# Raw steps loaded ahead, a split pool and a first cell with a pool of its own in a four-layer graph kernel

## The chip, the cores and the metric

The kernel runs on one core of a Trainium2 chip. The metric is the device time of one execution in microseconds (us). Engines are named as in the profile: PE (TensorE, matmuls; PEld its weight loads), DVE (VectorE), ACT (ScalarE), POOL (GpSimd) and SP (SyncE, which here only issues DMAs). A name followed by "q" (SPq) is the issuing queue of that engine.

## What is computed

A graph of 2708 nodes with 256 features passes through four layers; each adds the layer's output to its input and normalizes the row. The adjacency matrix `adj` is sparse in values, dense in storage (2708 x 2708, float32). Cut to what matters here:

```python
x = layernorm(x + adj @ (x * W0))                      # layer 0
# layer 1: attention with 4 heads of 64
e    = leaky_relu(src[:, None] + dst[None, :], 0.2)
attn = softmax(where(adj > 0, e, -9e15))
out1 = layernorm(attn @ h)
x    = layernorm(x + out1)
# layer 2: two GRU cells over sums and attention with signs
node_support = (adj - diag) @ x
edge_output  = gru(node_support, x, edge_Wih, edge_Whh)
edge_support = mean over 3 heads of (softmax by signs of adj) * adj @ (x @ gat_W)
node_output  = gru(edge_support, x, node_Wih, node_Whh)
x = layernorm(x + diag * edge_output + diag * node_output)
# layer 3
x = layernorm(x + concat(x, adj @ (x @ nW.T) / deg) @ lW.T)
```

The change touches the last part of layer 1 and the first part of layer 2: the sums `(adj - diag) @ x` and the first GRU cell that uses them.

## The kernel before

The nodes make 22 row tiles of 128 (the last has 20 rows). Features are kept as two parts of 128. Tiles of memory come from pools that are stacked on a left and a right side; a pool that is opened after another was closed takes its place, and what writes first into the new tile waits for the last use of the old one. Each engine's queue runs in order. A scheduler decides the order within each engine from the order of the program and the dependencies; `issue_after` holds some of it fixed (the p's on DVE behind each other, the head and total products on PE behind each other).

**Layer 1.** The loop at line 790 goes over groups of two spans of columns (`spans` are of up to 512 columns); the last group has 384 + 276 = 660 columns. Inside, the loop at line 813 goes over the two pairs of heads (q = 0 and 1), and for each pair over blocks of two tiles. DVE makes the attention weights `p` (line 844) from `fall_b`, a table of 128 x 2 x 1024 values for this group and pair that SP loads (line 417), from `rise` and from the mask; nine buffers (`held`) rotate. PE then multiplies: `heads` (line 820) gives the weighted sums in `acc`, `totals` (line 830) the denominators in `den`. Blocks alternate which of the two comes first.

`fall_b` is one of two buffers of the pool `fallp`, popped from the list `falls`; behind a group's last use a new tile of the same tag is appended and loaded for the next group.

Between the products, `step` (line 798) advances the ends of the tiles of the group before, two tiles (a pair) at a time. These are generators; each `yield` gives way to the next part of the products. `layer1_end` (line 687) turns the sums with PE transposes (lines 698, 699), divides by the denominators (DVE L709/L712, ACT L716), takes the variance and its power on POOL (L684), and adds and normalizes twice (DVE L731, L734; ACT L747, L748). `layer1_logits` (line 752) then transposes the new rows (PE L760), copies them out of PSUM (ACT L762), stores them to memory (POOL's DMA queue, L770), gives way once, and multiplies them with a small matrix (`pm`, PE L777: 128 x 3 outputs) whose result ACT copies to `u_all` (L781).

The last group has no group behind it that could cover its ends: they run from line 889 on, between the first raw steps.

**Raw sums.** `raw_sums` (line 354) is a generator for one "raw", a column block of 226 columns out of each half of the nodes (six raws; the last is 224 wide); `ahead` chains all of them. A raw has MH = 11 steps c, one for each pair of row tiles. A step loads four quarters of the adjacency matrix into a tile `pa` (`load_pairs`, line 259: five DMAs in raw 0, six in raw 1, all issued by SP), clears the diagonal where it falls (`clear_own`, POOL L286), and calls `seven` (line 309): four additions on DVE (L315 to L318) and seven products of block matrices on PE (L328, 14 matmuls, as the profile counts two for each float32 product). In raw 0 the step also forms `xq` from x (`quarter_sums`, DVE L294 to L297). Step c thus needs x of the tiles 2c and 2c + 1, and the last steps of raw 0 need x of layer 1's last group. At the end of a raw `gathered` (line 332) makes `supt`.

**Logits and first cell.** Lines 899 to 1055 form layer 2's attention logits and their statistics, with raw steps drawn from `ahead` between (`next(ahead)`). Their small tiles are in the pool `tail`, right side. At the end, PE transposes the statistics (L1044), ACT copies them (L1048) and POOL's queue stores them to `st_d` (L1054). Then the pools of layer 1 are closed, and the cells begin at line 1105: the pool `e_work` holds the weights `wih` and `whh`, the input `xt2` (two buffers) and what the cell works with. For each raw r the loop first draws raw steps until two raws are ready ahead, then loads the input and calls `gru_t` (line 1068): per half (j), 24 gate matmuls (L1081) into four PSUM banks, ACT's gate functions (L1086), DVE's combination (L1093 to L1099).

The stage behind it (line 1336 on) shares the engines with the later cells: ACT forms attention weights from the statistics that were stored (`st` loaded by SP at L1144; ACT L1347, L1350), DVE multiplies them with the adjacency block (L1351).

Of the kernel before, what the change touches and what calls it, by code (L numbers as in the profile page):

```python
# [9 lines left out]
F32 = mybir.dt.float32  # L10
# [9 lines left out]
P = 128  # L20
# [7 lines left out]
def kernel(  # L28
# [323 lines left out]
    xq = []  # L352

    def raw_sums(pool, ps, keep, r):

        a, w = raws[r]
        m = [ps.tile([P, 2, W // 2], F32, tag=nm, name=nm) for nm in ("m1", "m26", "m75", "m43")]
        m[0] = m[0][:, 0]
        for c in range(MH):
            pa = pool.tile([P, 2, 2, w], F32, tag="pa", name="pa", bufs=5)  # L360
            load_pairs(raws, r, c, pa)
            clear_own(raws, r, c, pa)
            if r == 0:
# [33 lines left out]

    keep_stack, fall_stack, acc_stack, ps_t_stack, xq_stack, eblk_stack, ps_s_stack = (ExitStack() for _ in range(7))
    keep = keep_stack.enter_context(pool("l1keep"))
    if True:  # L400
# [12 lines left out]
        if True:  # L413
# [39 lines left out]
            with pool("l0", 2) as l0:  # L453
# [165 lines left out]
                beta_b = keepr.tile([P, F], F32, name="beta_b")  # L619
                fallp = fall_stack.enter_context(pool("fallp", 2, side="right"))  # L620
                falls = [fallp.tile([P, 2, 2 * W], F32, tag="fall_b", name="fall_b") for _ in range(H // 2)]
                held = [fallp.tile([P, 2 * W], F32, name=f"p{i}", bufs=1) for i in range(4)]
# [42 lines left out]
            if True:  # L665
# [85 lines left out]

                def layer1_logits(pair):

                    pt = ps_t.tile([P, 4, P], F32, tag="tr", name="tr")
                    at = (2 * GT + 1 + 2 * (pair[0][-1] // 2 % 2)) * F
                    xt = turn[:, at : at + 2 * F].rearrange("p (i f n) -> p i f n", i=2, f=FC)
                    for i, a in enumerate(pair):
                        t, n = a[0], sz(a[0])
                        for f in range(FC):
                            nc.tensor.transpose(pt[:, i * FC + f, :n], xs[t][:n, f * P : (f + 1) * P], ident[:n, :n])  # L760
                    if all(sz(a[0]) == P for a in pair):
                        nc.scalar.copy(xt.rearrange("p i f n -> p (i f) n"), pt)  # L762
                    else:
                        for i, a in enumerate(pair):
                            n = sz(a[0])
                            nc.scalar.copy(xt[:, i, :, :n], pt[:, i * FC : (i + 1) * FC, :n])
                    for i, a in enumerate(pair):
                        t, n = a[0], sz(a[0])
                        at, _, d = [p for p in xt_d if p[0] <= t * P][-1]
                        nc.gpsimd.dma_start(d[:, :, t * P - at : t * P - at + n], xt[:, i, :, :n])  # L770
                    yield

                    pm = ps_t.tile([P, 4, P], F32, tag="tr", name="pm")
                    for i, a in enumerate(pair):
                        n = sz(a[0])
                        for f in range(FC):
                            nc.tensor.matmul(  # L777
                                pm[:n, i, :K], xt[:, i, f, :n], uw[:, f, :], start=(f == 0), stop=(f == FC - 1)
                            )
# [10 lines left out]
                for g in range(0, len(spans), 2):  # L790
# [7 lines left out]
                    def step(c):  # L798
                        with tc.issue_after(product.ins) if g == 0 else nullcontext():
                            for s in list(steps):  # L800
                                if next(s, s) is s:
                                    steps.remove(s)

                        if q == 0 and c % 5 == 1 and len(halves) < len(ended):
                            halves.append(layer1_end(l1, ended[len(halves)]))
                            next(halves[-1])
                            steps.append(itertools.islice(halves[-1], 2))

                        if q == 1 and c % 5 == 0 and c // 5 < len(halves):
                            steps.append(itertools.chain(halves[c // 5], [None], layer1_logits(ended[c // 5])))  # L810
                            next(steps[-1])

                    for q in range(H // 2):
# [21 lines left out]

                        fall_b = falls.pop(0)
                        for b, c0 in enumerate(range(0, NT, 2)):
# [18 lines left out]
                        if g + 2 < len(spans):  # L856
                            falls.append(fallp.tile([P, 2, 2 * W], F32, tag="fall_b", name="fall_b"))
                            for i in range(len(spans[g + 2 : g + 4])):
                                load_fall(falls[-1], g + 2 + i, q, nc.sync)
                        got = []  # L860
# [28 lines left out]
                turns = [itertools.chain(layer1_end(tail, a), [None], layer1_logits(a)) for a in ended]  # L889
                k = 0  # L890
# [7 lines left out]

                u_parts = tail.tile([P, NT, CT], BF16, name="u_parts", bufs=1)
                nc.gpsimd.memset(u_parts, 0.0)  # L900
                rest = u_all
                for i in range(SPLITS):
                    part = u_parts[:, :, i * K : (i + 1) * K]
                    nc.vector.tensor_copy(part, rest)
                    if i + 1 < SPLITS:
                        r = tail.tile([P, NT, K], F32, tag="u_left", name="u_left")
                        nc.vector.tensor_tensor(r, rest, part, ALU.subtract)
                        rest = r
# [15 lines left out]
                def turned_sums(acc, groups, cols, copies):  # L924

                    w, full = width(*spans[groups[0]]), len(groups) * cols
                    parts = tail.tile([P, W], F32, tag="parts", name="parts")
                    nc.scalar.copy(parts[:full, :w], acc[:full, :w])
# [22 lines left out]
                first = -STEP  # L951
                own_u = tail.tile([P, NT, K], F32, name="own_u", bufs=1)
                nc.vector.scalar_tensor_tensor(
# [5 lines left out]

                inside = tail.tile([P, NT, K], F32, name="inside", bufs=1)  # L960
                nc.vector.tensor_scalar(inside, logit, first - STEP / 2, None, ALU.is_ge)
# [14 lines left out]
                centres = centre[:, None].to_broadcast([P, NT, BANDS, K])  # L976
                q_parts = tail.tile([P, NT, 2 * CT], BF16, name="q_parts", bufs=1)
                nc.gpsimd.memset(q_parts, 0.0)
# [747 lines left out]
```

## Time and profile before

| | |
|---|---|
| times of three runs | 1844.74, 1841.54, 1843.25 us; median 1843.25 |
| the profiled execution | 1845.3 us; span from first to last instruction 1843.5 us |
| mean granted clock of PE in it | 0.997 of full speed |
| PE busy, 529 to 556 / 556 to 582 / 582 to 612 us | 27.00 of 27 / 24.45 of 26 / 26.78 of 30 |
| DVE busy in the same stretches | 26.04 / 15.24 / 26.60 |
| granted clock in the same stretches | 1.00 / 0.93 / 1.00 |
| layer 1's last pm before the passage, and the first tile transpose | 581.97 and 582.89 us |
| first cell's gate matmuls | begin at 708.69 us |

The profile is of one execution. A line of the timeline or of a group names the line of the kernel, the engine, the operation with its output and input, its shape, and how often it came (x); in square brackets stands how long the engine was idle before it and what released it. "L777" is line 777 of the kernel. Releasers are inferred; an end of a matmul is modelled, as matmuls are pipelined, so a short wait of PE can be hidden in a longer matmul, and "issue" is idle time with no releaser in the profile. The granted clock is the share of the full clock that TensorE was allowed in that stretch.

### The profile page before, as it was taken

The page shows a single profiled execution, that of the slowest core. Times are in us where ns is not written, and L with a number is a line of the kernel's source. Part 1 is how long each engine was busy: PE and PEld are TensorE (multiplying, and loading weights), DVE is VectorE, ACT ScalarE, POOL GpSimd, SP SyncE. Part 2 cuts the span into 40 slices and gives each one's busy share as a digit, 9 for nine tenths or more (in the row PEclk, how much of TensorE's full clock was granted, in tenths as well). Part 3 has the DMA queues.
Part 4 walks back from the last instruction along what each step waited for, and adds up shares of the span by engine and source line. Part 5 has one row for each costly group of instructions (what it writes and reads, how often), then busy time and mean ns, then how long its engine had stood idle before and what let it go on. Part 6 is the DMA issues. An engine that isn't in the chain of part 4 may idle for free.

```text
span 1843.5 us, 23048 instructions
## 1 busy us (share of the span) xinstructions
PE 1819.7 (99%) x7512; PEld 1038.2 (56%) x7512; DVE 1267.9 (69%) x2242; ACT 699.0 (38%) x1449; POOL 287.3 (16%) x441
## 2 busy tenths in 40 slices
PE   9999999999999999999999999999999999999997
PEld 7888842233455886788444444444445556655555
DVE  5333399998797655654558888686887768945664
ACT  4444420033144203111555655555654556321011
POOL 1322211011113411000002000110200202121211
PEclk9999999999999999999999999999999999999999
DMA  8343310000103667755557666453654445634774
GB/s 302 121 163 126 126 53 26 24 1 21 33 7 78 147 145 193 170 134 123 175 136 207 178 175 173 125 151 110 170 161 125 124 108 148 174 99 120 202 172 124
DMA packets 435711, 237.34 MB, mean 129 GB/s; under 512 B 184459, under 2 KB 422444, under 8 KB 433148
## 3 DMA queue, kind: packets, MB, share of 16 engines
q1 hardware_dynamic: 423534, 210.76, 42.3%
q0 software_dynamic: 7696, 20.50, 3.5%
q10 hardware_dynamic: 4350, 4.50, 0.7%
q8 instruction: 62, 1.02, 0.2%
q14 instruction: 69, 0.57, 0.1%
HBM read 223.00 MB, written 12.66 MB: 128 GB/s over the span
## 4 chain that ended last, share of the span: by engine, by line
PE 91%; DMA 3%; DVE 2%; ACT 1%; SPq 1%; issue 1%; POOL 0%; POOLq 0%; DVEq 0%
PE m L328 42%; PE acc L820 11%; PE acc L214 8%; PE bank L1206 8%; PE den L830 6%; PE gate L1081 4%; PE bank L1182 3%; PE bank L1249 2%; PE acc L519 2%; PE pm L425 1%; DMA strip<-in_adj_t_dram 1%; SPq L275 1%; PE m L1453 1%; DMA p<-in_adj_t_dram 1%; PE pq L1002 1%
## 5 line engine op out<-in xcount | busy, mean ns | idle before, releaser
L844 DVE SCALAR_TENSOR_TENSOR p<-fall_b,rise,mask 128x1024 f32<-128x1024 f32 (+1 forms) x264 | 288.5, 1154 | 28.8 <-PE den L830 17.4
L1347 ACT ACTIVATE p<-st,e_neg 128x1024 f32<-128x1024 f32 (+1 forms) x198 | 197.5, 1040 | 193.0 <-PE m L328 188.1
L328 PE MATMUL m<-s,xq 128*128 128x512 f32 (+3 forms) x660 | 230.1, 467 | 0.0
L820 PE MATMUL acc<-p,h 128*64 128x512 f32 (+2 forms) x1056 | 209.2, 546 | 0.0
L214 PE MATMUL acc<-turn,strip 128*128 128x257 f32 x792 | 182.8, 381 | 1.8 <-DMA strip<-in_adj_t_dram 1.7
L328 PE MATMUL m<-p,xq 128*128 128x512 f32 (+1 forms) x396 | 183.0, 544 | 0.2
L315 DVE TENSOR_TENSOR s<-p 128x512 f32<-128x512 f32 (+3 forms) x132 | 82.1, 622 | 146.8 <-PE m L328 115.1
L1350 ACT ACTIVATE p<-p 128x1024 f32<-128x1024 f32 (+1 forms) x198 | 179.0, 943 | 0.2
L328 PE MATMUL m<-p,x 128*128 128x512 f32 (+1 forms) x396 | 167.6, 542 | 0.3 <-DVE supt L345 0.3
L328 PEld LDWEIGHTS m<-s,xq 128*128 128x128 f32 x660 | 124.5, 190 | 76.1 <-issue 59.5
L1351 DVE TENSOR_TENSOR p<-p,blk 128x1024 f32<-128x1024 f32 (+1 forms) x132 | 142.9, 1102 | 34.4 <-ACT p L1350 23.4
L214 PEld LDWEIGHTS acc<-turn,strip 128*128 128x128 f32 x792 | 147.2, 189 | 23.7 <-DMA strip<-in_adj_t_dram 3.0
L820 PEld LDWEIGHTS acc<-p,h 128*64 128x64 f32 x1056 | 72.3, 137 | 129.3 <-issue 121.6
L328 PE MATMUL m<-s,x 128*128 128x512 f32 (+3 forms) x330 | 127.0, 467 | 0.0
L328 PEld LDWEIGHTS m<-p,xq 128*128 128x128 f32 x396 | 74.6, 190 | 76.9 <-issue 61.0
L328 PEld LDWEIGHTS m<-p,x 128*128 128x128 f32 x396 | 74.8, 190 | 75.5 <-issue 60.9
L457 DVE TENSOR_SCALAR mask<-strip 128x2816 fp8e4<-128x2816 f32 (+5 forms) x40 | 40.0, 1030 | 110.3 <-DMA strip<-in_adj_t_dram 110.2
L830 PE MATMUL den<-p,h 128*32 128x512 f32 (+2 forms) x1056 | 111.5, 551 | 0.0
L286 POOL TENSOR_TENSOR blk<-blk,offdiag 128x128 f32<-128x128 f32 (+3 forms) x50 | 29.1, 588 | 375.2 <-DMA blk<-in_adj_t_dram 326.3
L472 ACT ACTIVATE below<-strip 128x384 bf16<-128x384 f32 x132 | 78.4, 594 | 17.8 <-DMA strip<-in_adj_t_dram 14.4
L328 PEld LDWEIGHTS m<-s,x 128*128 128x128 f32 x330 | 62.0, 190 | 39.0 <-issue 34.6
L316 DVE TENSOR_TENSOR p<-p 128x512 f32<-128x512 f32 (+3 forms) x132 | 81.9, 620 | 2.4
(286 smaller groups left out, 2642.4 us busy)
## 6 DMA issues: line engine op xcount, KB each, us to landing
strip<-in_adj_t_dram SPq DMA_DIRECT2D x19, 1408.0 KB, 6.0
blk<-in_adj_t_dram SPq DMA_DIRECT2D x88, 256.0 KB, 3.5
blk<-in_adj_t_dram SPq DMA_DIRECT2D x88, 192.0 KB, 4.1
pa<-in_adj_t_dram SPq DMA_DIRECT2D x110, 128.0 KB, 2.7
turn<-in_adj_t_dram SPq DMA_DIRECT2D x44, 256.0 KB, 3.2
blk<-in_adj_t_dram SPq DMA_DIRECT2D x88, 128.0 KB, 2.7
p<-in_adj_t_dram SPq DMA_DIRECT2D x88, 128.0 KB, 2.8
turn<-in_adj_t_dram SPq DMA_DIRECT2D x44, 192.0 KB, 3.2
```

What stands on the lines that cost most here:

```text
L214: at = nc.tensor.matmul(acc, s[:, c, :n], rhs(c), start=(c == 0), stop=(c == NT - 1))
L315: nc.vector.tensor_tensor(s1, a21, a22, ALU.add)
L316: nc.vector.tensor_tensor(a21, a21, a11, ALU.subtract)
L328: nc.tensor.matmul(dst[:, :w], lt, rt, start=start and not (one_bank and i in (3, 4, 6)), stop=stop and not (one_bank and i in (1, 2, 5)))
L472: nc.scalar.activation(below[:, : (hi - lo) * P], s[:, lo:hi].rearrange("p c n -> p (c n)"), AF.Relu, scale=-1.0, accum_out=negative[:, BE ...
L820: at = nc.tensor.matmul(acc[s][i * HD : (i + 1) * HD, :ws], hs[c][:, 2 * q + i, :HD], ps[i][:, p0 : p0 + ws], **flags,)
L830: at = nc.tensor.matmul(den[j : j + CT, :ws], hs[c][:, 2 * q + i, HD + 1 - CT :], ps[i][:, p0 : p0 + ws], **flags,)
L844: nc.vector.scalar_tensor_tensor(p[:, :w], fall_b[:, i, :w], rise[:, c, 2 * q + i : 2 * q + i + 1], mask[:, c, at : at + w], ALU.max, ALU. ...
L1206: nc.tensor.matmul(g[:, :w], lt, rt, start=(q == 0), stop=(q == len(terms) - 1))
L1347: nc.scalar.activation(p[:, :, :w], st_k[:, :, :w], AF.Relu, scale=-1.0, bias=e_neg[:, at, k : k + 1])
L1350: nc.scalar.activation(p[:, :, :w], p[:, :, :w], AF.Exp, scale=-1.0)
L1351: nc.vector.tensor_tensor(p[:, :, :w], p[:, :, :w], blk[:, i, :, :w], ALU.mult)
```

## The change

- The two buffers of `fallp` become two tiles in two pools, `spare` for the first pair of heads and `fallp` for the second; each is loaded again for each group (`falls[q]`) instead of being allocated again.
- In the last group, after the first pair of heads, the first buffer isn't loaded again. Its first part becomes two views of the shape of `pa` (`early`), and raw steps 0 and 1 of raw 0 are loaded and cleared there at once (`loaded`). Of five buffers in rotation, two are these views from then on, and the pool of `pa` has three instead of five. For the cells, two tiles of `e_work` take the views' place.
- `layer1_logits` gives way twice instead of once before `pm` when it is called in the last group.
- The pool `tail` is split: the tiles of the logits' first part, the ends of layer 1 and several of the logits' sums come from a second pool `sums`, the rest (the band tiles, `centre`, `total`, `shift`, `den`, `drows`, `sr`) stays.
- `wih`, `whh` and the first `xt2` are in a pool `e_in` of their own, opened before `e_work`; the second `xt2` stays in `e_work`. For a raw with a cell, the input is loaded before the raw steps are drawn, not behind them.

The instructions are the same in number and kind apart from these places. In the order of PE, the cell's first gate matmuls come after 2 products of raw sums behind the transpose `pl` (L1061) where they came after 23, and the raw sums that no longer stand before it follow after the first half of the cell.

```diff
+    early, loaded = [], {}
+
+    def raw_loaded(pool, r, c):
+        if (r, c) in loaded:
+            return loaded.pop((r, c))
+        k = (r * MH + c) % 5
+        pa = early[k] if k < len(early) else pool.tile([P, 2, 2, RW], F32, tag="pa", name="pa", bufs=3)
+        load_pairs(raws, r, c, pa)
+        clear_own(raws, r, c, pa)
+        return pa
...
         for c in range(MH):
-            pa = pool.tile([P, 2, 2, w], F32, tag="pa", name="pa", bufs=5)
-            load_pairs(raws, r, c, pa)
-            clear_own(raws, r, c, pa)
+            pa = raw_loaded(pool, r, c)
...
-                fallp = fall_stack.enter_context(pool("fallp", 2, side="right"))
-                falls = [fallp.tile([P, 2, 2 * W], F32, tag="fall_b", name="fall_b") for _ in range(H // 2)]
+                spare = spare_stack.enter_context(pool("spare", side="right"))
+                fallp = fall_stack.enter_context(pool("fallp", side="right"))
+                falls = [a.tile([P, 2, 2 * W], F32, name=f"fall{q}") for q, a in enumerate((spare, fallp))]
...
-                def layer1_logits(pair):
+                def layer1_logits(pair, apart=1):
...
-                    yield
+                    for _ in range(apart):
+                        yield
...
-                            steps.append(itertools.chain(halves[c // 5], [None], layer1_logits(ended[c // 5])))
+                            steps.append(itertools.chain(halves[c // 5], [None], layer1_logits(ended[c // 5], 1 + (g + 2 >= len(spans)))))
...
-                        fall_b = falls.pop(0)
+                        fall_b = falls[q]
...
                         if g + 2 < len(spans):
-                            falls.append(fallp.tile([P, 2, 2 * W], F32, tag="fall_b", name="fall_b"))
                             for i in range(len(spans[g + 2 : g + 4])):
-                                load_fall(falls[-1], g + 2 + i, q, nc.sync)
+                                load_fall(fall_b, g + 2 + i, q, nc.sync)
+                        elif q == 0:
+                            free = fall_b.rearrange("p i n -> p (i n)")[:, : 8 * RW]
+                            early += list(free.rearrange("p (k j h n) -> k p j h n", k=2, j=2, h=2))
+                            for c in range(2):
+                                loaded[0, c] = raw_loaded(None, 0, c)
...
                 tail = fall_stack.enter_context(pool("tail", 2, side="right"))
+                sums_pool = fall_stack.enter_context(pool("sums", 2, side="right"))
...
-                logit = tail.tile([P, NT, K], F32, name="logit", bufs=1)
+                logit = sums_pool.tile([P, NT, K], F32, name="logit", bufs=1)
...
-    for q in (fall_stack, mask_stack, ps_t_stack):
+    for q in (fall_stack, spare_stack, mask_stack, ps_t_stack):
         q.close()
...
-    with pool("e_work") as ework, pool("ps_g", 4, space=PSUM, side="right") as ps_g:
-        wih, whh = weights(ework, "wih", e_wih), weights(ework, "whh", e_whh)
+    with pool("e_in") as e_in, pool("e_work") as ework, pool("ps_g", 4, space=PSUM, side="right") as ps_g:
+        early.clear()
+        inputs = [e_in.tile([P, FC, 2 * RW], F32, name="xt2")]
+        wih, whh = weights(e_in, "wih", e_wih), weights(e_in, "whh", e_whh)
+        inputs.append(ework.tile([P, FC, 2 * RW], F32, name="xt2"))
         for r, (a, w) in enumerate(raws):
+            if r not in left:
+                xt = inputs[r % 2][:, :, : 2 * w]
+                for h in range(2):
+                    load_columns(xt[:, :, h * w : (h + 1) * w], xt_d, h * NH + a, w)
+            if r == 1:
+                early[:] = [ework.tile([P, 2, 2, RW], F32, name=f"pa{i}") for i in range(2)]
             while len(edges) < min(r + 2, len(raws)):
                 next(ahead)
             if r not in left:
-                xt = ework.tile([P, FC, 2, w], F32, tag="xt2", name="xt2", bufs=2)
-                for h in range(2):
-                    load_columns(xt[:, :, h], xt_d, h * NH + a, w)
                 yt = ework.tile([P, FC, 2 * w], F32, tag="yt", name="yt")
-                gru_t(ps_g, ework, yt, edges[r], xt.rearrange("p f h w -> p f (h w)"), 2 * w, wih, whh, b_edge)
+                gru_t(ps_g, ework, yt, edges[r], xt, 2 * w, wih, whh, b_edge)
```

More of the change, by code (lines that the diff above doesn't have):

```diff
@@ L395 @@
     nc.gpsimd.memset(mask[:, :, N:], 0.0)
-    keep_stack, fall_stack, acc_stack, ps_t_stack, xq_stack, eblk_stack, ps_s_stack = (ExitStack() for _ in range(7))
+    keep_stack, spare_stack, fall_stack, acc_stack, ps_t_stack, xq_stack, eblk_stack, ps_s_stack = (ExitStack() for _ in range(8))
     keep = keep_stack.enter_context(pool("l1keep"))
@@ L887 @@
                 ahead = itertools.chain.from_iterable(raw_sums(eblk, ps_s, xqp, r) for r in range(len(raws)))
-                turns = [itertools.chain(layer1_end(tail, a), [None], layer1_logits(a)) for a in ended]
+                turns = [itertools.chain(layer1_end(sums_pool, a), [None], layer1_logits(a)) for a in ended]
                 k = 0
@@ L897 @@
                     k += 1
-                u_parts = tail.tile([P, NT, CT], BF16, name="u_parts", bufs=1)
+                u_parts = sums_pool.tile([P, NT, CT], BF16, name="u_parts", bufs=1)
                 nc.gpsimd.memset(u_parts, 0.0)
@@ L905 @@
                     if i + 1 < SPLITS:
-                        r = tail.tile([P, NT, K], F32, tag="u_left", name="u_left")
+                        r = sums_pool.tile([P, NT, K], F32, tag="u_left", name="u_left")
                         nc.vector.tensor_tensor(r, rest, part, ALU.subtract)
@@ L926, in turned_sums @@
                     w, full = width(*spans[groups[0]]), len(groups) * cols
-                    parts = tail.tile([P, W], F32, tag="parts", name="parts")
+                    parts = sums_pool.tile([P, W], F32, tag="parts", name="parts")
                     nc.scalar.copy(parts[:full, :w], acc[:full, :w])
@@ L951 @@
                 first = -STEP
-                own_u = tail.tile([P, NT, K], F32, name="own_u", bufs=1)
+                own_u = sums_pool.tile([P, NT, K], F32, name="own_u", bufs=1)
                 nc.vector.scalar_tensor_tensor(
@@ L958 @@
                 nc.vector.tensor_scalar(e_neg, logit, -1.0, None, ALU.mult)
-                inside = tail.tile([P, NT, K], F32, name="inside", bufs=1)
+                inside = sums_pool.tile([P, NT, K], F32, name="inside", bufs=1)
                 nc.vector.tensor_scalar(inside, logit, first - STEP / 2, None, ALU.is_ge)
@@ L976 @@
                 centres = centre[:, None].to_broadcast([P, NT, BANDS, K])
-                q_parts = tail.tile([P, NT, 2 * CT], BF16, name="q_parts", bufs=1)
+                q_parts = sums_pool.tile([P, NT, 2 * CT], BF16, name="q_parts", bufs=1)
                 nc.gpsimd.memset(q_parts, 0.0)
```

## The prediction

> **What bounds the kernel now.** I read the page's engine shares first, then PE's waits over the stretch that the change touches, then PE's timeline there, then the queues behind those waits.
>
> ```profile
> PE 1819.7 (99%) x7512; PEld 1038.2 (56%) x7512; DVE 1267.9 (69%) x2242; ACT 699.0 (38%) x1449; POOL 287.3 (16%) x441
> ...
> PE 91%; DMA 3%; DVE 2%; ACT 1%; SPq 1%; issue 1%; POOL 0%; POOLq 0%; DVEq 0%
> ```
>
> PE is busy 1819.7 of 1843.5 us, so only 23.8 us are idle in all. The change removes no matmul; it can win idle PE time, time hidden inside modelled matmul ends, and a lowered clock. PE's waits from 500 to 700 us:
>
> ```profile
> PE m L328 <- issue: 1.6, 2, 1.3
> PE pm L777 <- ACT turn L762: 1.5, 1, 1.5
> PE tr L698 <- ACT turn L716: 0.6, 1, 0.6
> PE m L328 <- DVE pa L316: 0.5, 1, 0.5
> PE m L328 <- POOL pa L286: 0.4, 1, 0.4
> ```
>
> All five lie in two places: one pm wait at 558, and the passage from layer 1 to the raw steps (583 to 612). PE's timeline at the first, then one-us windows over it (length, PE busy, granted clock, DMA):
>
> ```profile
> 556.53 1.35 PE L830 MATMUL den<-p,h 128*32 128x320 f32 x16
> 559.43 1.26 PE L777 MATMUL pm<-uw,turn 128*128 128x3 f32 x8 [1.55 <-ACT turn L762]
> 560.62 2.50 PE L830 MATMUL den<-p,h 128*32 128x320 f32 x16
> ```
>
> ```profile
> 558.00:559.00 1.00, 0.00 (x0) 1.00 0.00 0
> ...
> 560.00:561.00 1.00, 1.00 (x9) 0.57 0.12 41
> 561.00:562.00 1.00, 1.00 (x12) 0.50 0.70 213
> 562.00:563.00 1.00, 1.00 (x8) 0.50 0.03 8
> 563.00:564.00 1.00, 1.00 (x8) 0.72 0.00 0
> ```
>
> The reader sees a 1.55 us wait, and then the same 16 den matmuls taking 2.50 us instead of 1.35, at half clock. The copy L762 was ready at 556.53, but ACT held it behind L747, which waited until 557.4 for POOL's power; it ended at 559.38.
>
> At the second place (PE, then SP's queue):
>
> ```profile
> 585.96 1.19 PE L328 MATMUL m<-pa,x 128*128 128x226 f32 x4 [0.40 <-POOL pa L286]
> ...
> 607.18 0.62 PE L328 MATMUL m<-pa,xq 128*128 128x226 f32 x2 [1.26 <-issue]
> ...
> 611.84 0.60 PE L760 MATMUL tr<-ident,x 128*128 128x128 f32 x4
> ```
>
> ```profile
> 582.21 47.92 SPq L275 DMA_DIRECT2D pa<-in_adj_t_dram  x88
> ```
>
> SP issues loads back to back: 47.92/88 = 0.54 us each, five a step in raw 0, so 2.7 us a step; PE's step is 14 matmuls of 0.191 (four start 0.77 apart in the timeline) = 2.68. PE can't gain on SP, which starts only when layer 1's memory is free. No view says more for the next 300 us: PE's waits from 700 to 900 are 1.0 us.
>
> **The change, part by part.**
>
> *Second advance for pm (apart = 2 in the last group).* One totals part of the next block (1.28 to 1.35) moves from behind pm to before it: it fills 557.88 to 559.16, and pm then waits at most 559.38 − 559.16 = 0.22. Its p's were ready at 555.9 (DVE idles for PE at 564), so nothing else is late. Idle gain 1.28. At the group's other two logits (548, 571) pm didn't wait; there the order changes at no cost. Then the clock. The Trainium skill ("TensorE: Matmul & The Clock Gate", Part 1, HAM oscillation) has as its rule that only PE gaps above some 3.4 us drop the clock. By it the gap of 1.55 is harmless, the slow stretch belongs to something else, and this part is worth 1.3. The windows show 0.57, 0.50, 0.50, 0.72 right behind the gap; the lost full-speed time is 0.43+0.50+0.50+0.28 = 1.7, and by durations pm +0.2, den +1.15, acc +0.2 = 1.6. Gaps of 0.62 and 1.26 later did not drop it (clock 1.00 over 582 to 612). I take the trace: a gap of 0.2 drops nothing. **−2.9**, ends −1.3 and −3.1.
>
> *Two steps loaded early.* The ten loads go to SP's queue after the last q = 0 p has read the buffer (about 530), where SP waited 98 us for layer 1's end: free. Their POOL clears (two of 0.5) fall near 534, before the power of 536.5: hidden; if that cover goes, a power is 1 us later, which the ends of layer 1 have as slack everywhere but at 558. At the passage, PE's order becomes two tile transposes, step 0, two transposes, step 1, and so on, and DVE (idle 6.9 us up to 583.45) has step 0's sums ready. SP begins with step 2 at 582.2, while PE needs it 2 x 2.68 + transposes later: with 2.7 to land, each step is there some 2.5 us ahead. Before, 582.89 to 611.84 = 28.95 us held 8 steps (21.4) and the tile transposes (2.0): 5.6 lost, of which 3.2 show as waits. The 1.26 among them is POOL's clear of one step queued behind two powers (2.55); the clears of the same steps now stand ahead of those powers. Next limit: DVE, 26.6 busy of the 30 us to 612, and in order, so a tile end that waits for POOL's power holds up the next step's sums. I leave 0.6 for it: x of the first pair is turned at 606.9 instead of 611.84. **−4.9**, ends −2 (DVE sets the pace) and −5.6 (nothing lost).
>
> *Three pa buffers and two views instead of five.* Same count; the two reused views come up at steps 5 and 6, as buffers 0 and 1 did. Between the logits and the second cell three buffers rotate alone; a load may still be three steps (8.0 us) ahead, and needs 6 x 0.54 + 2.7 = 5.9. Nothing.
>
> *Tail split in two, weights and xt2 in a pool of their own.* No instruction is added or removed. wih, whh and the first xt2 no longer wait for the last logits store, so the first cell moves: before, PE ran 23 matmuls of raw sums after the last small transpose, then a half cell (24 gate matmuls); now 21 fewer come first, about 8 us. The work is the same, what stands in the queues is not. ACT: the node stage's first four L1347 and two L1350 (4 x 1.04 + 2 x 0.94 = 6.0) now stand ahead of the first gate activation, and wait for the st load, which reads what POOL stored at 691 to 698.
>
> ```profile
> 711.93 0.64 ACT L1086 ACTIVATE g_r<-gate,bcol 128x452 f32<-128x452 f32 x1 [3.07 <-DVE s L315]
> ...
> 724.67 1.15 ACT L1347 ACTIVATE p<-st,e_neg 128x1024 f32<-128x1024 f32 x1 [2.51 <-DMA st<-st]
> ```
>
> Here g_r ran 4.7 us before the first L1347, and L1347 4.7 us after the st load was issued (719.94). The order reverses. SP issues that load once the stores have landed, about 695.3; plus 4.7 is 700, plus 6 and waits 706.7 for g_r. PE has four gate banks, a half cell of 24 x 0.379 (from L1081's rows) = 9.1 us, begins near 700.7 and first needs a bank back at 709.8: 3 us of slack. What is late next is DVE: two L1351 (1.1 each) and a step's sums that wait for their DMA stand before the cell's first operation, and the next raw steps' sums behind the cell's (0.63 to 0.72 each). No row of before shows the cell in this order; from nothing lost (all covered) to two L1351 and one landing late (2.2 + 1). A gain isn't excluded, as PE's waits here were about 0, but it could be only tenths. I take half: **+1.5**, ends 0 and +3.
>
> **Sum.** −2.9 − 4.9 + 1.5 = −6.3. The profiled execution took 1845.3 with a span of 1843.5, 1.8 around it: its span becomes 1837.2 and its time 1839.0. It stands 2.05 above the median of 1843.25, so the median goes to **1837.0**.
>
> **Rivals.**
>
> *DVE bounds the passage.* For it: 26.6 busy of 30. Against: 6.9 us of idle before 583 take the first sums. Then −2 there: −2.9 − 2 + 1.5 = −3.4, so 1839.8, about no change. With no clock gain as well (−1.3) 1841.5. Chance 0.17.
>
> *The loads were not the limit, nor does the clock return* (the change doesn't do what it says: PE waits for the tile ends anyway, and the half clock comes from another cause). Only pm's 1.3, less 1.5: 1843.4. For it: 2.4 of the 5.6 lost never show as waits. Chance 0.05.
>
> *ACT's queue at the first cell.* The st load lands later than 703 (more than 3 us over my sum), because SP stands behind the stores and loads share the memory; L1347, six operations and g_r follow in order, all four gate banks are full, PE stands still. From 3 us on each us counts, and a gap like the 1.55 above adds 1.6 of half clock. A landing 12 us late costs 9 + 1.6; with −7.8 from the other parts it's +2.8, 1846. It turns the sign at 9.2 us late. For it: the load moves to just behind the stores. Against: the largest landing seen for st is 4.6. Chance 0.08.
>
> Forecast: 0.70.
>
> **How the numbers follow.** Two times of this kernel can be told apart from about 0.2%, 3.7 us; below 1839.55 is faster, above 1846.95 slower. The forecast's own terms, at their ends, run from 1843.25 − 3.1 − 5.6 = 1834.5 to 1843.25 − 1.3 − 2 + 3 = 1843; a range of 1833.8 to 1842 takes in the first rival and nearly all of the forecast. Faster: the forecast's 0.70 but for 0.06, plus 0.08 of the first rival, 0.72. Slower: of the third, 0.06, for what exceeds its turning point well. Same: 0.22.
>
> **What would show it.** Right: no wait at pm near 558 and granted clock 1.00 up to 570; step 0 between the tile transposes, no L328 waits to 607, and x of the first pair turned 4 to 5 us sooner against the last pm of layer 1; early loads near 530. At the cell: L1347 before the first g_r, PE gaps under 3 us together. Wrong: PE waits for DVE sums through the passage; a clock below 1 that stays near 560; a gate matmul waiting for ACT, with L1347 released by the st load.

## The result and the profile after

The changed kernel takes 1838.55 us (median of 22 runs, 1836.78 to 1841.20) beside 1843.26 us of the kernel before (22 runs): ratio 0.9974, 95% interval 0.9968 to 0.9980, or 4.7 us less. Predicted were 6.3. The profiled execution lost 6.2 us of span (1843.5 to 1837.3), as predicted nearly to the tenth; the steps show that this agreement is partly chance. PE's waits from 500 to 700 us, after:

```profile
PE pm L788 <- ACT turn L772: 0.9, 1, 0.9
PE gate L1097 <- DVE one L1079: 0.9, 1, 0.9
PE m L328 <- issue: 0.6, 1, 0.6
```

None of the five waits of before is left in its place, and three stand in new ones: a raw step at 596, the pm at 608 and the first gate matmul at 695. (Lines have moved: L777 is now L788, L760 L770, L762 L772, L684 L694, L1081 L1097.) The first place, PE's timeline after:

```profile
556.21 2.49 PE L841 MATMUL den<-p,h 128*32 128x320 f32 x32
558.63 1.05 PE L788 MATMUL pm<-uw,turn 128*128 128x3 f32 x8
559.62 4.66 PE L831 MATMUL acc<-p,h 128*64 128x384 f32 x32
```

The 32 den matmuls run in one piece and pm follows without a wait. The granted clock is 1.00 in every slice of one us from 554 to 565. The passage, PE and then SP, POOL and ACT:

```profile
580.07 0.93 PE L328 MATMUL m<-fall,x 128*128 128x226 f32 x4
...
596.26 0.62 PE L328 MATMUL m<-fall,xq 128*128 128x226 f32 x2 [0.58 <-issue]
...
604.11 0.60 PE L770 MATMUL tr<-ident,x 128*128 128x128 f32 x4
...
608.28 1.05 PE L788 MATMUL pm<-uw,turn 128*128 128x3 f32 x8 [0.90 <-ACT turn L772]
```

```profile
573.94 8.56 SPq L275 DMA_DIRECT2D pa<-in_adj_t_dram  x15
```

```profile
599.30 7.51 POOL L694 TENSOR_TENSOR o_rs<-o_var,neg_half 128x1 f32<-128x1 f32 x2 [1.82 <-DVE o_var L693]
```

```profile
606.84 0.29 ACT L757 ACTIVATE o_mean<-o_mean,o_rs 20x1 f32<-20x1 f32 x1 [5.43 <-POOL o_rs L694]
...
607.67 0.56 ACT L772 COPY turn<-tr 128x512 f32<-128x512 f32 x1
```

Step 0 (its buffer is named `fall`) begins behind the transposes of two tiles. From the first of these (579.38) to the transposes of the last group's first new rows (604.11) it takes 24.73 us instead of 28.95. But then pm waits 0.90 for ACT's copy, which stands behind an ACT operation that waited for POOL: the last two powers took 7.51 us. It is the old pattern of 558 at a new place. The first cell, PE and ACT:

```profile
695.34 1.78 PE L1097 MATMUL gate<-xt,whh 128*128 128x452 f32 x4 [0.88 <-DVE one L1079]
...
719.82 0.65 PE L328 MATMUL m<-pa,xq 128*128 128x226 f32 x2 [0.67 <-DVE pa L316]
```

```profile
695.32 2.19 ACT L1369 ACTIVATE p<-st,e_neg 128x1024 f32<-128x1024 f32 x2 [3.42 <-DMA st<-st]
...
701.38 0.62 ACT L1102 ACTIVATE g_r<-gate,bcol 128x452 f32<-128x452 f32 x1
```

**Where the 6.2 us of the profile are.** I set the start of the same instruction in both traces side by side; the difference grows or shrinks between them.

| up to | before | after | saved since the row above |
|---|---|---|---|
| tr before pm, layer 1 (L760, L770) | 555.95 | 555.62 | 0.3 |
| first tile transpose of the passage | 582.89 | 579.38 | 3.2 |
| transposes of the last group's new rows | 611.84 | 604.11 | 4.2 |
| last gate matmul of the early cells (start of its four) | 842.2 | 837.2 | -2.7 |
| first matmul of the late gates (L1206, L1228) | 889.7 | 885.4 | -0.6 |
| last product of layer 3 | 1833.0 | 1828.3 | 0.3 |
| end | 1843.5 | 1837.3 | 1.5 |

### The profile page after: what moved, and what is told of

It reads as the page before. It is cut to its first block, busy times and chain, and to the rows that moved or that the text cites. A ratio compares the mean times of both kernels' runs of the same rounds, so it can differ in the third digit from the quotient of the medians.

```text
span 1837.3 us, 23072 instructions
## 1 busy us (share of the span) xinstructions
PE 1818.2 (99%) x7512; PEld 1037.5 (56%) x7512; DVE 1265.9 (69%) x2242; ACT 699.5 (38%) x1449; POOL 294.6 (16%) x441
## 4 chain that ended last, share of the span: by engine, by line
PE 89%; DMA 4%; ACT 2%; issue 1%; DVE 1%; SPq 1%; POOL 1%; POOLq 0%; DVEq 0%; ACTq 0%
PE m L328 41%; PE acc L831 11%; PE acc L214 8%; PE bank L1228 8%; PE den L841 6%; PE bank L1204 3%; PE gate L1097 3%; PE bank L1271 2%; PE acc L528 2%; PE pm L434 1%; DMA strip<-in_adj_t_dram 1%; PE m L1475 1%; PE pq L1018 1%; SPq L275 1%; ACT p L1369 1%
## 5 line engine op out<-in xcount | busy, mean ns | idle before, releaser
L855 DVE SCALAR_TENSOR_TENSOR p<-fall,rise,mask 128x1024 f32<-128x1024 f32 (+1 forms) x264 | 288.9, 1154 | 24.3 <-PE den L841 17.0
```

The costliest lines, as they stand in the source:

```text
L855: nc.vector.scalar_tensor_tensor(p[:, :w], fall_b[:, i, :w], rise[:, c, 2 * q + i : 2 * q + i + 1], mask[:, c, at : at + w], ALU.max, ALU. ...
```

## The experiments

Ratios are to runs of the kernel before on the same chip, with 95% intervals; the chips differ among each other by some us, so only ratios are compared.

**The parts alone.** Four kernels: pm moved, and nothing else; the early loads alone; the pools of the cell alone; and the first two together, without the pools.

```diff
-                    yield
+                    for _ in range(apart):
+                        yield
```

(The diff shows the main place of the first one; `apart` is 2 in the last group and 1 elsewhere. The others are parts of the diff of the whole change.)

> The kernel before, with pm moved behind one more part of the products in layer 1's last group, and nothing else. My theory: PE's gap of 1.55 us before that pm caused the half clock behind it, so both go: no wait over 0.3 us at pm, the granted clock 1.00 from 552 to 582, and the first tile transpose of the passage at 582.9 - 3.2 = 579.7 (within 0.4). All later stalls stay as they were, so the time falls by about 3.0 us (1840.2). Rival (the half clock comes from something else, such as the burst of stores at 561): clock below 1 again near 561, the first transpose near 581.4, 1841.7. Second rival (the time won here is lost at the next wait): the transpose earlier, but the first transposes of the last group's new rows at 611.8 still.

Measured: 0.9984 (0.9978 to 0.9991), 2.9 us less. The timeline of its PE:

```profile
555.36 2.49 PE L831 MATMUL den<-p,h 128*32 128x320 f32 x32
557.78 1.05 PE L778 MATMUL pm<-uw,turn 128*128 128x3 f32 x8
...
578.53 0.42 PE L698 MATMUL tr<-ident,sum 128*128 128x128 f32 x2
```

No wait stands at pm, and the granted clock is 1.00 from 552 to 582. The first transpose of the passage is at 578.53, 4.36 us earlier; of this 1.18 was there before the place (the transposes at 555.95 stand at 554.77 in this profile), so 3.18 come from it, as much as in the changed kernel. So the half clock went with the gap.

> The kernel before, with steps 0 and 1 loaded in layer 1's last group and the two tables in two pools, but pm and the first cell as before. My theory: the wait before pm (about 1.5 us) and the half clock behind it stay; the passage from the first tile transpose to the transposes of the last group's new rows falls from 28.95 to 24.7 (within 0.5), and of these 4.2 us about 1.2 are given back at the first pm behind it, which waits for ACT's copy; net 3.0, so 1840.2. Rival (my prediction's size): 4.9 won and nothing given back, 1838.4. Rival (the passage is bound by DVE before too): at most 2, 1841.3.

Measured: 1.0031 (1.0019 to 1.0043), 5.7 us **more**. The passage is as expected, 581.75 to 606.49 (24.74), and pm near 611 waits 0.9. What nobody expected stands at the first cell, in the list of PE's waits:

```profile
PE gate L1095 <- DMA xt<-xt: 6.3, 1, 6.3
```

> The kernel before, with the split pool and the first cell's weights and input in a pool of their own, nothing else. My theory from the trace of the changed kernel: a wait of about 0.9 us for DVE's L1079-like reduction before the first gate matmul, 1.3 us in the raw steps behind the half cell (about as much as the same steps lose elsewhere in the kernel before) and 0.5 for the input of a later cell: 1.0 to 1.6 us slower than before, 1844.5. Rival (my prediction): ACT and DVE hold up the cell by 1.5, not the bank. Rival (the pool is what pays): faster than before by over 1 us, and the sum of the other two parts alone falls short of the whole change.

(The "L1079-like reduction" is the one of `one`, L1064 there.) Measured: 1.0010 (1.0002 to 1.0018), 1.8 us more, with 1.65 us of wait for that reduction.

> The changed kernel without its pools for the cell: pm moved and two steps loaded early, first cell as before. My theory: the parts add up, 3.2 + 3.0 = 6.2 us less than before, 1837.0, and about 1.5 less than the changed kernel (1838.55): faster than both. Rival (the cell's pool takes away a wait that the other two parts create, such as loads that stand behind the late weights): equal to or slower than the changed kernel.

Measured: 1.0014 (1.0005 to 1.0023), 2.6 us more than before, so some 7 more than the changed kernel. My theory that the parts add up has fallen; what happened is the rival named in that expectation. The timeline of this kernel, PE and SP, and then SP of the changed kernel:

```profile
703.24 3.35 PE L1096 MATMUL gate<-xt,whh 128*128 128x452 f32 x4 [6.87 <-DVE s L318]
706.38 2.62 PE L1096 MATMUL gate<-supt,wih 128*128 128x452 f32 x4
```

```profile
693.28 0.41 SPq L222 DMA_DIRECT2D wih<-in_L_gnn_edge_Wih_dram  x1
693.86 0.37 SPq L222 DMA_DIRECT2D whh<-in_L_gnn_edge_Whh_dram  x1
695.21 2.20 SPq L257 DMA_DIRECT2D xt<-xt  x3
```

```profile
673.01 0.41 SPq L222 DMA_DIRECT2D wih<-in_L_gnn_edge_Wih_dram  x1
...
681.71 2.21 SPq L257 DMA_DIRECT2D xt<-xt  x3
```

The first gate waits 6.87 us and then runs four matmuls in 3.35 instead of 1.68, at half clock. The releaser that the line names is DVE, whose work was long done; the kernel with the early loads alone names the true one, the input `xt`. Here it was issued from 695.21 on and landed 6.5 to 7.1 us later, the last piece at 703.10, and the gate began at 703.24. It was issued late because SP's queue runs in order: a load of the statistics ahead of it waited 2.5 us for the logits' stores to land, and a step's loads and the weights stood between. The windows from 695 to 700 (length, PE busy, clock, DMA share, GB/s) of this kernel and of the changed one show that much is loaded at once in this one:

```profile
695.00:700.00 5.00, 1.36 (x8) 1.00 1.07 379
```

```profile
695.00:700.00 5.00, 4.66 (x13) 1.00 0.81 195
```

But that costs the input little: behind the weights it took 6.3 us to land in the changed kernel too, and 6.1 to 6.6 in the kernel before. What differs is when it is issued and when it is needed. In the kernel before, the same loads were as late (wih at 699.46, the input landed at 707.9), but PE had 23 products (in the program's count) of raw sums to do first, until 708.69. With the early loads the scheduler places the cell 7 products behind the last small transpose. In the changed kernel the weights go out from 673.01 and the input at 681.71, 20 and 13.5 us earlier than here.

**Is it the place of the cell?** The same kernel (without the pools), with the cell's matmuls ordered behind three more raw steps; the diff shows the two main places.

```diff
+                if r == 0:
+                    next(ahead), next(ahead), next(ahead)
...
+                    with tc.issue_after(after.ins) if after is not None else nullcontext():
```

> The changed kernel without its pools for the cell (as the run before it, which lost 6.9 us at the first gate matmul and 2.6 at half clock behind it), but with the first cell's gate matmuls held behind three more raw steps, so that 21 products in the program's count follow the last small transpose and not 7. My new theory: what the early loads do alone is to let the scheduler put the cell right behind the last transpose, while its weights still wait for the memory of the last logits store; 14 more products are 28 x 0.191 = 5.3 us of cover, so the wait at the first gate falls from 6.9 to about 1.5, the clock stays at 1.00, and the time is 5 to 7 us below the run without the hold, that is 3.5 to 6 below the kernel before. Rival (the weights are late because the loads themselves crowd each other, wherever the cell stands): the wait at the first gate stays above 4 us, and the time is that of the kernel before or above.

Measured: 1.0006 (0.9999 to 1.0012). It is no different from the kernel before. The wait at the gate is gone, but its time isn't: the raw steps that were put ahead wait themselves. PE, and DVE ahead of the first of these waits:

```profile
701.46 1.08 PE L330 MATMUL m<-pa,xq 128*128 128x226 f32 x2 [2.84 <-DVE pa L318]
...
708.50 1.12 PE L330 MATMUL m<-pa,xq 128*128 128x226 f32 x2 [2.41 <-DVE pa L318]
```

```profile
697.84 2.36 DVE L1374 TENSOR_TENSOR p<-p,blk 128x1024 f32<-128x1024 f32 x2 [3.15 <-ACT p L1373]
700.12 0.39 DVE L317 TENSOR_TENSOR s<-pa 128x226 f32<-128x226 f32 x1
```

Half clock follows each wait. They aren't waits for loads: the loads of the first step had landed at 697.6, and those of the second by 702.6. What came late is DVE. In its order, two multiplications of the node stage (L1374, L1351 before) stand ahead of the first step's sums, and they had waited for ACT until 697.84; at the second step DVE worked without a break from 697.84 until it came to these sums at 707.15. So neither side of that expectation holds. The cover brought the input in time, as the theory said, and the crowd of loads of the rival cost nothing more at the gate; but the node stage on DVE, which in the kernel before begins behind the first cell's gates, holds up the steps that should have covered. With memory of their own the inputs need no such cover: in the changed kernel they go out 13.5 us earlier than without it, and the raw steps behind the cell wait only 0.67 and 0.33 us. Whether the three buffers left to the raw loads matter was not tried.

**The waits left in the changed kernel.**

```diff
-            if r == 0:
+            if r == 0 and c >= len(xq):
...
+                xq.extend(quarter_sums(xqp, xs, c, "xq") for c in range(4))
```

> The changed kernel with the quarter sums of steps 0 to 3 formed ahead of the passage, in DVE's idle time before 578, so that DVE has 2.4 us less to do in the passage. My theory: DVE sets the pace there (1.3 us lost), and its unbroken run of additions with two inputs from memory holds up POOL's last power (6.4 us instead of 0.5 to 2.3), which makes ACT's copy and the pm at 608 late by 0.9. With gaps in DVE's work the passage to the transposes of the new rows falls from 24.7 to under 24.2, the last power takes under 4 us and the pm waits under 0.4: 0.5 to 2 us less than the changed kernel, that is 5 to 7 below the kernel before. Rival (POOL's power is slow for a reason of its own): the power still takes over 5 us, and nothing is won at the pm. Second rival: the hoisted sums delay step 0 instead, and PE waits at 580.

Measured: 0.9972 (0.9965 to 0.9978), no different from the changed kernel. Of the theory only the pm's wait came out, at 0.35, and it won nothing: the two last powers still took 6.98 us (now it is the first of them that is held, for 6.47), and a gap of 1.51 us opened at 600 in a raw step, so that the passage took 25.4 us instead of 24.7. The first rival is what happened.

```diff
-                turns = [itertools.chain(layer1_end(sums_pool, a), [None], layer1_logits(a)) for a in ended]
+                turns = [itertools.chain(layer1_end(sums_pool, a), [None], layer1_logits(a, 2)) for a in ended]
```

> The changed kernel with pm held one more part behind the transposes in the passage too, where it waits 0.9 us for ACT's copy behind POOL's late power. My theory: the same cure as in the last group takes this wait away (1.2 us with what hides in the matmul's end), and the first cell moves seven products closer to the last small transpose, which makes its wait for DVE's reduction longer by up to 1 us: between 1 less and 0.5 more than the changed kernel. Rival: the whole 1.2 is won. Second rival: the input of the cell isn't there yet, and a wait of more than 2 us stands at the first gate.

Measured: 0.9964 (0.9952 to 0.9977), 6.6 us below the kernel before. All of PE's waits of this kernel from 500 to 730 us:

```profile
PE m L328 <- DVE pa L316: 1.3, 1, 1.3
PE m L328 <- issue: 0.6, 1, 0.6
PE gate L1097 <- DVE one L1079: 0.4, 1, 0.4
```

The pm's wait is gone as expected. The wait at the first gate shrank too, where I had expected it to grow; a raw step behind the cell waits longer (1.3). It is the lowest ratio of all; but against the changed kernel (0.9974, and 0.9971 on another chip) the intervals overlap, so that it beats the changed one is not shown.

The third kernel moved the transpose `pl` and the reduction behind it ahead of the statistics' transposes.

> The changed kernel with the maximum, its transpose pl and its reduction on DVE placed ahead of the statistics' transposes. In the changed kernel the first gate matmul waits 0.9 us for that reduction (DVE L1079), which stands behind a step's sums, as the gates' banks take the memory of the bank it reads. My theory: this wait goes, 1.0 us less than the changed kernel, 5.7 below the kernel before. Rival: the gate then waits as long for the next thing in line (ACT's copy of the statistics from the same banks, or the cell's input), and the time is that of the changed kernel.

Measured: 0.9977 (0.9971 to 0.9984). The wait at the gate is gone, and one of 2.15 us (with half clock behind it) stands in the raw steps behind the cell instead. So it was that reduction that the gate waited for, but the 1.0 us wasn't won: the cell starts earlier, and the steps' sums on DVE are late by more.

```diff
+        if gap:
+            nc.vector.tensor_scalar(a21[:, :2], a21[:, :2], 1.0, 0.0, ALU.mult, ALU.add)
```

> The changed kernel with one small DVE instruction more in each of raw 0's last five steps: a multiplication by 1 of two columns, which reads a single tensor, between the additions of two tensors. Nothing else moves. My theory: POOL's last power takes 6.4 us because DVE runs only two-tensor operations from 601 to 606.4 without a break, and POOL gets at its operand only when DVE doesn't read two tensors; with the small instruction in between it gets through at the next one: the last power under 3 us, ACT's copy earlier, the wait at the pm near 608 from 0.9 to under 0.3. Cost: five times some 0.15 us on DVE. Time: 0 to 1 us below the changed kernel. Rival (POOL is slow by itself there, or waits for DVE to stop for good): the last power still ends only when DVE goes idle, and the wait at pm stays or grows.

(`gap` is true in steps 6 to 10 of raw 0.) Measured: 0.9976 (0.9969 to 0.9982). The rival held; the wait at pm grew to 1.2. POOL and DVE of this run:

```profile
598.35 7.68 POOL L696 TENSOR_TENSOR o_rs<-o_var,neg_half 128x1 f32<-128x1 f32 x2 [1.81 <-DVE o_var L695]
```

```profile
607.02 0.29 DVE L295 TENSOR_TENSOR xq<-x,xq 128x128 f32<-128x128 f32 x1 [1.34 <-ACT x L760]
```

The powers ended at 606.03; DVE had gone idle at 607.02 - 1.34 = 605.68. Three of the small instructions (at 601.3, 603.4 and 605.5) fell within the power that was held.

> The small DVE instruction of the run before this one, and the pm in the passage one part later as well. If both cures work on the same wait, they don't add up: 6 to 7 us below the kernel before, as with the later pm alone. If the earlier power also shortens DVE's wait for the last rows (1.4 us near 608), a further 0.5 to 1.

Measured: 0.9966 (0.9952 to 0.9979), the same as the later pm alone.

> The kernel before once more, for its profile. The gap of 1.55 us before the pm near 559 is part of the program's order, so it must stand there again. Theory from the runs so far (a gap of this length was followed by half clock in two profiles and by full clock in one): whether the clock falls behind it is a matter of when the gap falls, so it may be full or half here; with half clock, the 16 den products behind pm take 2.5 us, without it 1.35. Rival (the gap always brings it): half clock.

Measured: 1843.31 us. The gap is there, 1.55 us, and the half clock too, but it sets in 2.3 us behind the gap (560.74) where it was 0.7 in the first profile (560.14): the 16 den products behind pm take 1.35, and the loss falls on the products behind them.

> The changed kernel beside the same runs of the kernel before as the two with the small instruction: 4 to 5.5 us below it. Its profile should show the same waits as the first one (0.9 at the pm near 608, 0.9 at the first gate), POOL's last power at 6 us or more, and the end of the program, where 1.5 us of the first profile's gain lay behind the last matmul, near the kernel before's: if that 1.5 is gone, the change had no part in it.

Measured: 0.9971 (0.9959 to 0.9983), 5.3 us less. The same waits (0.9 at the pm, 0.7 at the gate), POOL's powers 7.50. But the end is not that of the kernel before, as I had expected: it is as early as in the first profile (see the last section).

## Why the prediction was right in sum, and where its steps were not

**The pm in the last group: right, with a size that depends on the run.** Predicted -2.9; the profile shows 3.2, and the part alone 2.9 (interval 1.7 to 4.0). I weighed the threshold of some 3.4 us of the Trainium skill, named in the prediction, against the trace and took the trace. The runs bear out that shorter gaps can cost the clock, but not always. In the kernel with the cell's pools alone, the same gap of 1.55 is followed by full speed:

```profile
557.65 1.05 PE L777 MATMUL pm<-uw,turn 128*128 128x3 f32 x8 [1.55 <-ACT turn L762]
558.64 1.35 PE L830 MATMUL den<-p,h 128*32 128x320 f32 x16
```

The mean clock of each run fits this without a profile: of 42 runs of the kernel before on one chip, 24 had a mean clock of 0.997 or 0.996 and 18 of 0.998 or 0.999; at 0.997 the mean time is 1841.7, at 0.998 1839.8. All 22 runs of the changed kernel have 0.998 or 0.999. So, as an estimate from these counts, about half of the 1.6 us for the clock is in the median. This is one reason why the median fell less than the profiled pair.

**The early loads in the passage: right in mechanism, 0.7 short, and 1.2 given back.** Predicted 4.9, measured 4.2 in three kernels alike. The next limit was DVE, as named, but it cost 1.3 and not 0.6: the step at 596 waits for its sums (0.58, with what hides in the matmul's end 0.75), and another at 602. SP had more lead than I gave it: its first three steps for the small pool go out from 573.94, 5.4 us ahead of the first transpose. So I was wrong about SP's start, and it made no odds. (The waits of the passage that I put at 3.2 sum to 3.0 by their lines, which has no bearing.) The term that I put at nothing without a reason is the wait behind it: the pm near 608 (0.90, in all 1.2). "Where a stall goes, say what is late next" was answered with DVE, not with ACT's queue behind POOL, which I had just read off at 558.

**The pools: the sum near, the causes wrong.** I priced them at +1.5 (0 to +3), and that is what they cost alone: +1.8. In the changed kernel, too, about 1.9 us are lost at the cells: 1.05 at the first gate, 0.6 for an input at 885, and 0.2 net in the raw steps. But I had named other causes. What cost was the bank of the first gate, which had to wait for DVE's reduction of `pl` (0.88, in all 1.05), and that input; both were missed. What I named was there and cost little. The first L1347s stand before g_r, the st load (issued at 691.16) landed after 4.2 us, g_r ran at 701.38, and the bank was needed 9.2 us after 695.34, at 704.5: 3.1 us of slack, as worked out. The rival of ACT's queue thus fell. DVE's share was 1.7 us in the raw steps behind the cell (by their starts against the steady pace), but the kernel before lost 1.5 by the same reckoning in its own steps from 768 to 778.

The other fault is how I priced them. I put the cell's move down to the pools alone, and never asked what the early loads do to the cell without them. They move it as well (7 products behind `pl`, the pools 2), and with late inputs: early loads and pm give 1.0014 without the pools and 0.9974 with them, so the pools are worth some 7 us there. This doesn't bear on the sum, as the change has all three parts; but parts that share a queue don't have one price each.

One reading was wrong besides, in the description of the change as well: what I called a half cell of 24 gate matmuls in the order of PE is the whole first cell (24 in the program's count are 48 in the profile's), and the raw sums follow behind it. The slack for the gates' banks doesn't change by it.

**The rest is luck.** Of the 6.2 us of the profiled pair, 3.2 + 4.2 - 3.3 = 4.1 come from the steps that I priced, 0.6 from stretches that the change doesn't touch, and 1.5 lie behind the last matmul, which no step of mine reached. That end is as early in both profiles of the changed kernel; if it is so in all its runs, some 1.6 of the median's 4.7 us come from there, and only about 3.1 (an estimate) from PE's waits and clock, half of what I predicted. Shortfalls of 0.7 in the passage, 1.2 at pm and about 0.7 for the clock were in part made up by an end that I didn't foresee.

## What to carry to other kernels

When a stall is taken away, look for the next one in the same list of causes: an in-order queue that held up one result can hold up the next when the work arrives sooner. Parts of a change that share a queue aren't to be priced one by one; price the change with each part left out. Work that comes sooner also needs its inputs sooner: give them memory that is free long before, so that they can be issued well ahead of it.

## What the runs showed beside

**The end of the program.** From the issue of the last store (SP L1385, in after L1407) to the end it takes 7.5 to 7.6 us in the four profiles without the early loads (both of the kernel before, pm alone, the pools alone), and 5.4 to 6.1 in all ten with them. From 2.7 us behind that issue on, the DMA queues of before (first) and after show, up to the end,

```profile
q14 instruction: 4, 0.03, 2.4%
```

```profile
q14 instruction: 2, 0.02, 1.8%
```

and nothing else: two fetches of instructions fewer. All fourteen profiles fall in the same two groups. The records of POOL tell where the time lies. Behind its last branch POOL pauses 2.5 to 2.6 us in the four and 0.44 in the ten, and then a `DRAIN` instruction of 4.48 us follows in each, behind which the program ends within 0.8 to 1.5 us. The changed program has 24 instructions more than 23,048, so the branch may fall elsewhere in what is fetched. That the pause is a fetch was not tried.

**POOL beside DVE.** The last two powers of the passage (128 x 1 and 20 x 1 values) take 2.04 and 0.54 us before, and 1.14 and 6.40 after. This is POOL in the second profile of the kernel before, beside 7.51 after:

```profile
602.56 2.48 POOL L684 TENSOR_TENSOR o_rs<-o_var,neg_half 128x1 f32<-128x1 f32 x2 [1.60 <-DVE o_var L683]
```

In all fourteen profiles one of these two is held until 0.35 to 0.42 us after DVE went idle: after, DVE stopped at 606.39 and the power ended at 606.80; before, 604.98 and 605.40. DVE has to go idle there in any case, as its next operation waits for what comes out of POOL; but a power that ran by itself would not end so evenly behind it, whether held for 2 us or 6. The Trainium skill (GPSIMD Engine Reference, table of section 1) says that POOL's interfaces to memory are shared with DVE and contend with DVE's instructions that have two inputs there, or that run in a certain mode (it calls it a 2-port mode). This fits a DVE that ran additions of two tensors nearly without a break from 601 on. But three small operations on a single tensor within that time did not let POOL in (in which mode they ran, no profile tells), and other powers took 0.7 to 0.9 beside such additions. What POOL waits for stays open.

**The clock.** Gaps of PE with their sequel in all fourteen profiles: sixteen of 1.1 to 1.51 us, full clock each time; 1.55, half clock in three profiles of four; 1.65, once, full clock; 2.15 to 6.9, half clock each time (five gaps). Each stretch of half clock behind these gaps lasted 3.4 us, or 6.8 behind the gaps of 6.3 and 6.9. So the prediction's 1.6 to 1.7 us for one gap is half of 3.4. That only gaps above some 3.4 us count (the rule of the Trainium skill, TensorE: Matmul & The Clock Gate, Part 1, HAM oscillation) does not hold here; from 1.55 to 1.65 it depends on the run.
